# Graph convolution over 200,000 edges: feature parts stored once, a narrower spread of the source rows, and a zero fill moved from SP's queue to POOL's

## The chip, the cores and the metric

The kernel runs on one core of one Trainium2 chip. That core has five engines that run their own instruction streams: TensorE (PE, with its weight loads shown as PEld), VectorE (DVE), ScalarE (ACT), GpSimd (POOL) and SyncE (SP). SP computes nothing here; it issues most of the DMAs. POOL issues the DMAs that gather or scatter by index, and a few plain ones. The metric is the time of one execution in device microseconds (us), the median of several runs. Before the change it is 2110.86 us (three runs, 2110.19 to 2114.73).

## The reference: one message passing layer

There are 6250 nodes with 128 features each, and 200,000 edges. An edge has a source, a destination (the edges are sorted by it), 20 features and a weight. What is computed is, cut to its core:

```
h    = relu(layernorm(x))                      # 6250 x 128
xn   = h @ W_in                                # 6250 x 128
W_ij = (ssp(f_ij @ W_f1 + b_f1) @ W_f2 + b_f2) * cutoff     # one row of 128 per edge
m    = xn[dst] * W_ij                          # gather by idx_j = dst, 200,000 x 128
out  = segment_sum(m, idx_i = src, 6250)       # scatter-add by source
y    = x + ssp(out @ W_o1 + b_o1) @ W_o2 + b_o2
```

`ssp` is the shifted softplus, log(1+e^v) - log 2. The gather is by the sorted column, so it is local. The scatter-add is by the unsorted column, so it goes all over the 6250 rows.

## The kernel before, in words

**Quads.** The edges are cut in chunks of 128, and four chunks make a quad of 512 edges (391 quads). Two quads make a superchunk `s` of 1024 edges, the unit in which `load_sc(s)` (line 265) loads. The main loop (line 945) runs one iteration a quad, software pipelined by hand: iteration `i` does the first stage of quad `i`, the second of `i-1`, the scatter of `i-4`, and at even `i` issues `load_sc(i/2+2)`. Inside `manual_schedule` every engine executes its instructions in the order in which the Python code issues them. Work that happens only sometimes (preparing nodes, splitting features, zeroing, the permuted quads) hangs on hooks: `at(i, point, fn, ...)` puts it at a named point of iteration `i`.

**Edge filter.** For a quad, PE multiplies the split weights `ws` with the feature tile `ft` (`s1_pe`, L290). ACT and DVE make the softplus of it (L295 to L325), and PE multiplies by `W_f2` (L348). To keep float32 accuracy with bfloat16 products, every float32 feature is split into three bfloat16 parts (high, middle, low) and the weights likewise. `ft` has 6 groups of 20 rows: some parts of the features stand in it several times, beside different parts of the weights. Which weight part stands in which group is the table `part` (line 1267).

**The features' way.** Features are split in blocks of 4096 edges (49 of them; `fb_load`, `fb_1` to `fb_4`, L238 to L263). The result goes to the DRAM tensor `fsd` by three DMAs (L260 to L262), which store 6 copies: the high part three times, the middle part twice, the low part once. `load_sc` then reads `ft`, 120 rows of 1024 bfloat16, by one DMA (L271).

**Gather.** `wn` (L283) loads four windows of 21 rows, each with three bfloat16 parts, of the table of nodes `tab`, and a one-hot matrix made from `rb` (L276) picks rows out of them by a matmul (L340). ACT and DVE multiply with the filter to give the messages `m` (L353, L358).

**Scatter, two ways.** 60% of the quads, and all of the first eight, are *plain*: `sb` holds the row of source numbers spread over all 128 partitions (L273), DVE compares it with the sources as a column to get `eq` (L319), a matmul with `eq` (L370) adds up messages of the same source in a chunk, ACT copies the sum into one of five buffers `s` (L378), and POOL issues one scatter-add DMA a chunk, four a quad (L418). The other 40% (`mpi`: quads 8, 10, 13, 15, 18, 20 and so on) are *permuted*: they are sorted into bins by matmuls (L528) and added up in an on-chip accumulator `accT` by more matmuls (L621), with only one scatter-add for two quads. Permuted quads read no `sb`.

**Four accumulators.** Scatter-adds go to four DRAM accumulators in turn (`acc_of`, line 402): the first two scatters to accumulator 0, up to the eighth to 0 and 1, then to three and later to four. A scatter to an accumulator waits until the one before it to the same accumulator has landed. Before any of this an accumulator has to be zeroed, by ten DMAs of 320 KB (`zero_piece`, line 144). Accumulator 0 is zeroed by POOL (4 pieces at L674, 6 at L761). Accumulator 1 is zeroed by ten pieces that SP issues ahead of the main loop (L774). The pieces of accumulators 2 and 3 are spread over SP's first iterations.

**Queues.** SP executes its DMAs in order, and so does POOL. In the instruction listing a DMA of SP's gets one of eight semaphores in turn, so it also waits until the DMA eight places ahead of it has landed; the same holds for POOL's with eight semaphores of their own. One `load_sc` is 8 DMAs of SP's: `ft`, `sb`, two `rb`, four `wn`.

**The end.** After the loop a repair loop (L1008) runs zero times with these inputs. Then the three remaining accumulators are loaded (L1076), summed with `accT`, and go through the two output matmuls.

Of the kernel before, what the change touches and what calls it, by code (L numbers as in the profile page):

```python
# [8 lines left out]
BF16 = mybir.dt.bfloat16  # L9
# [11 lines left out]
P = 128  # L21
SC = 1024
SEG = 512
# [16 lines left out]
HB = 64  # L40
NR = 3 * WIN
NACC = 4
CQ = 16
EARLY_N = 256

# [2 lines left out]
def tile_gnn(ctx: ExitStack, tc: tile.TileContext, x, fB, cT, srcT, srcr, dstr, win_, wf1, wf2, bias, bo1c, wo1,  # L48
             wo2, consts, ident, out, n_edges):
    nc = tc.nc  # L50
    N = out.shape[0]
    NP = x.shape[0]
    NB, RB, BE = fB.shape
    EP = NB * BE
    KF = 6 * RB
    K1 = KF + 3
    FE = RB * BE // P
# [12 lines left out]
    ZR = 10 if ACC_R % 10 == 0 else 1  # L70
# [4 lines left out]
    mpi = {q: n for n, q in enumerate(mpq)}  # L75
# [12 lines left out]
    dp = ctx.enter_context(tc.tile_pool(name="dp", bufs=1, space=DRAM))  # L88
# [6 lines left out]
    accs = []  # L95
    for k in range(NACC):
        a_ = dp.tile([ACC_R, P], F32, name=f"acc{k}")
# [1 line left out]
    tab = dp.tile([NP * 3, P], BF16, name="tab")  # L99
    reld = dp.tile([NSC, SC], BF16, name="reld")  # L100
    src16 = dp.tile([NSC, SC], I16, name="src16")
    fsd = dp.tile([NB, 6, RB * BE], BF16, name="fsd")
    dropd = dp.tile([P, EP // P], BF16, name="dropd")

    con = cp.tile([P, 16], F32, name="con")
# [38 lines left out]
    def zero_piece(eng, k, j, parts=1):  # L144
        v = accs[k].rearrange("(p t) f -> p (t f)", p=P).rearrange("p (r e) -> r p e", r=ZR)
        w = ACC_R // ZR // parts
        for h in range(parts):
            eng.dma_start(v[j][:, h * w:(h + 1) * w], zero[:, :w])
# [107 lines left out]
    def fb_4(b):  # L256
        f3 = fst[b]["f3"]
        nc.vector.tensor_tensor(f3[:, 2], fst[b]["fr"], f3[:, 1], op=ALU.subtract)
        v = fsd[b].rearrange("g (p e) -> p g e", p=P)
        nc.sync.dma_start(v[:, 0:3], f3[:, 0:1].to_broadcast([P, 3, FE]))  # L260
        nc.sync.dma_start(v[:, 3:5], f3[:, 1:2].to_broadcast([P, 2, FE]))
        nc.sync.dma_start(v[:, 5:6], f3[:, 2:3])  # L262
        del fst[b]  # L263

    def load_sc(s):
        n = min(SC, NQ * SEG - s * SC)
        pp, hh, nh = s % HALF, s // HALF, n // SEG
        top = caps[s]
        ft = fts[s % len(fts)]
        b, o = s * SC // BE, s * SC % BE  # L270
        nc.sync.dma_start(ft[:KF, :n], fsd[b].rearrange("g (r e) -> (g r) e", r=RB)[:, o:o + n])  # L271
        sb = ld.tile([P, SC], I16, tag="sb", name="sb")
        nc.sync.dma_start(sb[:, :n], src16[s:s + 1, :n].to_broadcast([P, n]))  # L273
        rb = ld.tile([P, SEG], BF16, tag="rb", name="rb")
        for j in range(nh):
            nc.sync.dma_start(rb[j * HB:(j + 1) * HB], reld[s:s + 1, j * SEG:(j + 1) * SEG].to_broadcast([HB, SEG]))  # L276
        wn = ld.tile([P, 2, P], BF16, tag="wn", name="wn")
        _, regs = nc.values_load_multi_w_load_instructions(
            base_i[pp:pp + 1, hh, 0:2 * nh], engines=[SP], min_val=0, max_val=top,
            skip_runtime_bounds_check_because="clamped on the chip to [0, top]")  # L280
        for k in range(2 * nh):
            j, c = divmod(k, 2)
            nc.sync.dma_start(wn[j * HB:j * HB + NR, c, :], tab[bass.ds(regs[k] * 3, NR), :])  # L283
        loads[s] = (ft, sb, rb, wn)
# [367 lines left out]
    def c_load(b):  # L652
        n = min(4 * CQ, EP // P - 4 * CQ * b)
        t_ = ld.tile([P, 4 * CQ], F32, tag="cb", name="cb", bufs=2)
# [16 lines left out]
    with tc.manual_schedule():  # L671
# [88 lines left out]
        nc.gpsimd.tensor_copy(b2rep, b2p.unsqueeze(1).to_broadcast([P, 4, P]))  # L760
        for j in range(ZR * 4 // 10, ZR):  # L761
            zero_piece(nc.gpsimd, 0, j)
        ms = []
        for i in range(2):
            m_ = cp.tile([P, 4, 132], F32, name=f"m{i}")
# [5 lines left out]
            load_sc(1)  # L771
        if NB > 1:
            fb_load(1)
        for j in range(ZR):  # L774
            zero_piece(nc.sync, 1, j)

        hooks = {}

        def at(i, point, fn, *a):
# [228 lines left out]
    with tc.For_i(0, trips, 1) as ci:  # L1008
        dcol = wk.tile([P, 1], I32, bufs=1, tag="dcol", name="dcol")
        nc.sync.dma_start(dcol, dstr.rearrange("s (e o) -> (s e) o", o=1)[bass.ds(ci * P, P), :])  # L1010
        rcol = wk.tile([P, 1], BF16, bufs=1, tag="rcol", name="rcol")
        nc.sync.dma_start(rcol, reld.rearrange("s (e o) -> (s e) o", o=1)[bass.ds(ci * P, P), :])
        scol = wk.tile([P, 1], I32, bufs=1, tag="scol", name="scol")
        nc.sync.dma_start(scol, srcr.rearrange("s (e o) -> (s e) o", o=1)[bass.ds(ci * P, P), :])
        ccol = wk.tile([P, 1], F32, bufs=1, tag="ccol", name="ccol")
        nc.sync.dma_start(ccol, cT[:, bass.ds(ci, 1)])
        xcol = wk.tile([P, 1], BF16, bufs=1, tag="xcol", name="xcol")
        nc.sync.dma_start(xcol, dropd[:, bass.ds(ci, 1)])
        sb = wk.tile([P, P], I32, bufs=1, tag="oeq", name="fsb")
        nc.sync.dma_start(sb, srcr.rearrange("s e -> (s e)")[bass.ds(ci * P, P)].unsqueeze(0).to_broadcast([P, P]))  # L1020
        ft = wk.tile([P, P], BF16, tag="oh", name="fft")
        nc.vector.memset(ft[96:P, :], 1.0)
        fsel = fsd.rearrange("b g (r e) -> b (g r) e", r=RB)
        nc.sync.dma_start(ft[:KF, :], fsel[bass.ds(ci // (BE // P), 1), :, bass.ds((ci % (BE // P)) * P, P)]
                          .rearrange("o m e -> (o m) e"))
        x3 = wk.tile([P, 3, P], BF16, tag="pt", name="fx3")
        nc.gpsimd.indirect_dma_start(out=x3.rearrange("p k f -> p (k f)"), out_offset=None,
                                     in_=tab.rearrange("(n k) f -> n (k f)", k=3),
                                     in_offset=bass.IndirectOffsetOnAxis(ap=dcol[:, 0:1], axis=0))
        ok = wk.tile([P, 4], F32, bufs=1, tag="ok", name="ok")  # L1030
        nc.vector.tensor_scalar(ok[:, 0:1], rcol, float(WIN), None, op0=ALU.is_ge)
        nc.vector.tensor_scalar(ok[:, 1:2], rcol, 0.0, None, op0=ALU.is_lt)
        nc.vector.tensor_tensor(ok[:, 2:3], ok[:, 0:1], ok[:, 1:2], op=ALU.add)
        nc.vector.scalar_tensor_tensor(ok[:, 3:4], ok[:, 2:3], xcol, ccol, op0=ALU.max, op1=ALU.mult)
        xw = wk.tile([P, P], F32, bufs=1, tag="rm", name="fxw")
        nc.vector.tensor_tensor(xw, x3[:, 0], x3[:, 1], op=ALU.add)
        nc.vector.tensor_tensor(xw, xw, x3[:, 2], op=ALU.add)
        z = ps.tile([P, P], F32, tag="A", name="fz", bufs=4)
        nc.tensor.matmul(z, ws, ft[:K1, :], start=True, stop=True)
        e = wk.tile([P, P], F32, tag="e", name="fe")  # L1040
        nc.scalar.activation(e, z, AF.Abs)
        nc.scalar.activation(e, e, AF.Exp, scale=-1.0)
        nc.scalar.activation(e, e, AF.Ln, bias=half, scale=0.5)
        a = wk.tile([P, P], F32, tag="a", name="fa")
        nc.vector.scalar_tensor_tensor(a, z, 0.0, e, op0=ALU.max, op1=ALU.add)
        W = ps.tile([P, P], F32, tag="A", name="fW", bufs=4)
        nc.tensor.matmul(W, onesb[HB:], b2rep[HB:, 0, :], start=True, stop=False)
        nc.tensor.matmul(W, a, w2, start=False, stop=True)
        m = wk.tile([P, 132], F32, tag="xc", name="fm")
        nc.vector.tensor_copy(m[:, 128:129], wgt)  # L1050
        nc.vector.scalar_tensor_tensor(m[:, :P], W, ok[:, 3:4], xw, op0=ALU.mult, op1=ALU.mult)
        eq = wk.tile([P, P], F32, tag="eq", name="feq")
        nc.vector.tensor_tensor(eq, sb, scol.to_broadcast([P, P]), op=ALU.is_equal)
        pp = ps.tile([P, 132], F32, tag="B", name="fpp", bufs=4)
        nc.tensor.matmul(pp[:, :129], eq, m[:, :129], start=True, stop=True)
        s = wk.tile([P, P], F32, bufs=1, tag="dg", name="fs")
        nc.scalar.copy(s, pp[:, :P])
        dlt = wk.tile([P, 2], F32, bufs=1, tag="dlt", name="dlt")
        nc.vector.tensor_scalar(dlt[:, 0:1], scol, trash, None, op0=ALU.subtract)
        nc.vector.scalar_tensor_tensor(dlt[:, 1:2], pp[:, 128:129], wgt2, dlt[:, 0:1], op0=ALU.is_lt, op1=ALU.mult)  # L1060
        ji = wk.tile([P, 1], I32, bufs=1, tag="fji", name="fji")
        nc.vector.tensor_scalar(ji, dlt[:, 1:2], trash, None, op0=ALU.add)
        nc.gpsimd.indirect_dma_start(out=accs[1][:, :], out_offset=bass.IndirectOffsetOnAxis(ap=ji[:, 0:1], axis=0),
                                     in_=s, in_offset=None, compute_op=ALU.add)
# [172 lines left out]
def _layout(inputs):  # L1237
    import numpy as np

    p = "L0_gnn_"  # L1240
# [3 lines left out]
    n, e = x.shape[0], src.shape[0]  # L1244
# [19 lines left out]
    con[:, 14] = np_ // GRP // 2 - con[:, 3]  # L1264
    con[:n_sc // 2, 5] = caps[:n_sc // 2]
    con[:n_sc // 2, 6] = caps[n_sc // 2:]
    part = np.array([0, 1, 2, 0, 1, 0])
    for r in range(6 * rb + 3):
        con[r, 7 + (part[r // rb] if r < 6 * rb else r - 6 * rb)] = 1.0
    for r in range(3):  # L1270
# [39 lines left out]
```

## Time and profile before

| What | us |
|---|---|
| median of three runs | 2110.86 |
| the profiled execution | 2108.97 |
| its span, from the first instruction to the last | 2107.2 |
| PE busy in the span | 1926.4 (91%) |
| ACT busy | 1793.4 (85%) |
| DVE busy | 1774.3 (84%) |
| POOL busy | 1685.2 (80%) |
| share of the 16 DMA engines, SP's queue | 39.4% |
| share of the 16 DMA engines, POOL's queue | 34.8% |
| bytes moved | 314.79 MB |

The busy share of an engine is an average over the start (to about 110 us), the steady loop and the end (from about 2000 us), which have different limits. POOL's busy time leaves out the short stretch between two of its DMAs in which nothing is recorded as waited for; the idle column of its rows shows it. A row of a timeline gives start, duration, and in square brackets the idle time before it with what ended it. A wait for several things is put down to the one that came last.

### The profile page before, as it was taken

What the parts mean: (1) busy time and instruction counts of PE and PEld (TensorE: products, weight loads), DVE (VectorE), ACT (ScalarE), POOL (GpSimd) and SP (SyncE); (2) the same over time, 40 slices, a digit from 0 to 9 for tenths busy, and PEclk for the clock granted to TensorE, in tenths of its full rate; (3) what the DMA queues carried; (4) which work ended last, traced back from release to release, by engine and by line L of the source; (5) the groups of instructions that cost most, each with busy time, mean ns of one, the idle gap of its engine ahead of it and who ended that gap; (6) DMA issues with size and microseconds to landing.
All of it is one profiled execution on the core that took longest, in us unless ns stands there. A gap on an engine that the chain in (4) does not pass through costs nothing. (4 is left out here: it accounts for less than half of the span.)

```text
span 2107.2 us, 56868 instructions
## 1 busy us (share of the span) xinstructions
PE 1926.4 (91%) x19917; PEld 1402.2 (67%) x19917; DVE 1774.3 (84%) x4749; ACT 1793.4 (85%) x4789; POOL 1685.2 (80%) x1067
## 2 busy tenths in 40 slices
PE   3788999999999999999999999999999999999976
PEld 2566666676767666766666677777777766766644
DVE  4767888888889898888888989898988988888855
ACT  4687988898989898988889999989899889988824
POOL 2677878888888888888887888888888888888874
PEclk9888999999999999999999999999999999999997
DMA  7986767777777777777776777777777777777739
GB/s 266 237 179 126 153 133 144 135 155 137 152 136 154 141 140 147 152 141 141 152 142 140 144 140 135 152 140 150 137 152 149 142 138 143 138 132 161 138 39 240
DMA packets 394833, 314.79 MB, mean 149 GB/s; under 512 B 94863, under 2 KB 334266, under 8 KB 394546
## 3 DMA queue, kind: packets, MB, share of 16 engines
q1 hardware_dynamic: 245858, 240.57, 39.4%
q0 software_dynamic: 148400, 70.52, 34.8%
q8 instruction: 156, 2.56, 0.5%
q14 instruction: 131, 1.07, 0.2%
q10 hardware_dynamic: 288, 0.07, 0.0%
HBM read 173.32 MB, written 137.67 MB: 148 GB/s over the span
## 5 line engine op out<-in xcount | busy, mean ns | idle before, releaser
L418 POOL DMA_INDIRECT acc<-s,ji x948 | 1523.7, 1607 | 348.1 <-issue 225.6
L528 PE MATMUL pq<-pt,pm 128*128 128x387 bf16 x2464 | 487.0, 337 | 32.9 <-ACT s L378 18.7
L353 ACT ACTIVATE xc<-xg,cb 128x128 f32<-128x128 f32 x1564 | 446.5, 374 | 64.7 <-PE xg L340 50.1
L348 PE MATMUL W<-w,a 128*128 128x128 f32 x3128 | 462.5, 292 | 0.0
L348 PEld LDWEIGHTS W<-w,a 128*128 128x128 f32 x3128 | 386.9, 195 | 41.7 <-issue 2.0
L621 PE MATMUL un<-so,mst 32*128 32x392 bf16 x7392 | 359.4, 329 | 35.1 <-DVE pr L468 14.8
L528 PEld LDWEIGHTS <-pm 128*128 128x128 bf16 x2464 | 241.2, 98 | 195.3 <-issue 40.3
L621 PEld LDWEIGHTS <-mst 32*128 32x128 bf16 x7392 | 227.1, 94 | 162.3 <-issue 63.4
L325 DVE SCALAR_TENSOR_TENSOR a<-z,e 128x512 f32<-128x512 f32 x391 | 266.9, 683 | 64.9 <-ACT e L301 37.1
L301 ACT ACTIVATE e<-e,con 128x512 f32<-128x512 f32 x391 | 282.3, 722 | 12.7
L370 PEld LDWEIGHTS pp<-m,eq 128*128 128x128 f32 x1896 | 254.5, 196 | 32.6 <-DVE accT L632 13.7
L370 PE MATMUL pp<-m,eq 128*128 128x129 f32 x1896 | 260.8, 281 | 12.4 <-DVE accT L632 9.0
L534 ACT CAST mst<-pq 128x387 bf16<-128x387 f32 x616 | 264.2, 481 | 6.2 <-PE pq L528 4.7
L295 ACT ACTIVATE e<-z 128x512 f32<-128x512 f32 x391 | 241.7, 618 | 18.5 <-PE z L290 17.8
L296 ACT ACTIVATE e<-e 128x512 f32<-128x512 f32 x391 | 246.5, 630 | 12.4
L378 ACT COPY s<-pp 128x258 f32<-128x258 f32 x474 | 165.2, 391 | 91.2 <-DMA acc<-s,ji 34.4
L358 DVE TENSOR_TENSOR m<-W,xc 128x512 f32<-128x512 f32 x237 | 162.3, 685 | 69.7 <-ACT xc L353 49.6
L518 DVE TENSOR_TENSOR pt<-pt 128x512 f32<-128x512 f32 x308 | 212.5, 690 | 0.0
L504 DVE TENSOR_SCALAR pm<-iot,pos 128x576 bf16<-128x576 f16 x616 | 202.0, 389 | 0.0
L358 DVE TENSOR_TENSOR pt<-W,xc 128x512 f32<-128x512 f32 x154 | 105.9, 687 | 81.2 <-ACT xc L353 50.5
L632 DVE TENSOR_TENSOR accT<-un,accT 128x392 f32<-128x392 f32 x288 | 142.8, 557 | 36.9 <-PE un L621 26.2
L290 PE MATMUL z<-ft,ws 123*128 123x512 bf16 x391 | 152.2, 390 | 18.3 <-DMA ft<-fsd 18.3
(156 smaller groups left out, 2710.6 us busy)
## 6 DMA issues: line engine op xcount, KB each, us to landing
sb<-src SPq DMA_DIRECT2D x195, 256.0 KB
ft<-fsd SPq DMA_DIRECT2D x195, 240.0 KB
rb<-reld SPq DMA_DIRECT2D x391, 64.0 KB
fsd<-f SPq DMA_DIRECT2D x49, 480.0 KB
fb<-in_fB_dram SPq DMA_DIRECT2D x49, 320.0 KB
fsd<-f SPq DMA_DIRECT2D x49, 320.0 KB
acc<-s,ji POOLq DMA_INDIRECT x948
wn<-tab SPq DMA_DIRECT2D x782, 15.8 KB
```

Source lines behind the costliest of these rows:

```text
L295: nc.scalar.activation(e, st[q]["z"], AF.Abs)
L296: nc.scalar.activation(e, e, AF.Exp, scale=-1.0)
L301: nc.scalar.activation(e, e, AF.Ln, bias=half, scale=0.5)
L325: nc.vector.scalar_tensor_tensor(a, st[q]["z"], 0.0, st[q]["l"], op0=ALU.max, op1=ALU.add)
L348: nc.tensor.matmul(W[:, c, :], st[q]["a"][:, c * P:(c + 1) * P], w2, start=False, stop=(c == 3))
L353: nc.scalar.mul(xc[:, c, :], st[q]["xg"][:, c, :], late["c", q // CQ][:, 4 * (q % CQ) + c:4 * (q % CQ) + c + 1])
L358: nc.vector.tensor_tensor(m[:, :, :P], st[q]["W"], st[q]["xc"], op=ALU.mult)
L370: nc.tensor.matmul(pp[:, c, :129], st[q]["eq"][:, k, :], m[:, k, :129], start=True, stop=True)
L418: nc.gpsimd.indirect_dma_start(out=accs[k][:, :], out_offset=bass.IndirectOffsetOnAxis(ap=ji, axis=0), in_=s, in_offset=None, compute_op=A ...
L528: nc.tensor.matmul(t[:, :PW], mp[q]["pm"][:, c, s * P:(s + 1) * P], high(mp[q]["pt"][:, c:c + 1, :PW])[:, 0], start=(c == 0), stop=(c == 3))
L534: nc.scalar.copy(mp[q]["ms", s][:, :PW], mp[q].pop(("q", s))[:, :PW])
L621: nc.tensor.matmul(ts[g][:, :GN], mp[q]["ms", s][v, k * P:(k + 1) * P], mp[q]["oh"][v], start=(q == qs[0] and k == 0), stop=(q == qs[-1] a ...
```

## The change

Three edits are made together.

1. `fsd` holds each of the three feature parts once. `fb_4` writes them by one DMA of 480 KB instead of three of 480, 320 and 160 KB. `load_sc` reads `ft` by three DMAs of 60, 40 and 20 rows: parts 0 to 2, then 0 and 1, then 0. The groups of `ft` now stand in the order 0 1 2 0 1 0, so the weights' table is turned to `[0, 0, 0, 1, 1, 2]`. The repair loop's load is changed in the same way.
2. `sb` is loaded only over the columns of the plain quads of the superchunk: 512 columns where one of its two quads is permuted, 1024 where both are plain.
3. The ten zero pieces of accumulator 1 are issued by POOL, right behind its last pieces of accumulator 0, and no more by SP ahead of the loop.

```diff
+FPARTS = ((0, 3), (3, 2), (5, 1))
-    fsd = dp.tile([NB, 6, RB * BE], BF16, name="fsd")
+    fsd = dp.tile([NB, 3, RB * BE], BF16, name="fsd")
...
     def fb_4(b):
         f3 = fst[b]["f3"]
         nc.vector.tensor_tensor(f3[:, 2], fst[b]["fr"], f3[:, 1], op=ALU.subtract)
-        v = fsd[b].rearrange("g (p e) -> p g e", p=P)
-        nc.sync.dma_start(v[:, 0:3], f3[:, 0:1].to_broadcast([P, 3, FE]))
-        nc.sync.dma_start(v[:, 3:5], f3[:, 1:2].to_broadcast([P, 2, FE]))
-        nc.sync.dma_start(v[:, 5:6], f3[:, 2:3])
+        nc.sync.dma_start(fsd[b].rearrange("g (p e) -> p g e", p=P), f3)
         del fst[b]
...
-        nc.sync.dma_start(ft[:KF, :n], fsd[b].rearrange("g (r e) -> (g r) e", r=RB)[:, o:o + n])
+        for g, m in FPARTS:
+            nc.sync.dma_start(ft[g * RB:(g + m) * RB, :n],
+                              fsd[b, :m].rearrange("g (r e) -> (g r) e", r=RB)[:, o:o + n])
         sb = ld.tile([P, SC], I16, tag="sb", name="sb")
-        nc.sync.dma_start(sb[:, :n], src16[s:s + 1, :n].to_broadcast([P, n]))
+        own = [j for j in range(nh) if 2 * s + j not in mpi]
+        if own:
+            v = slice(own[0] * SEG, (own[-1] + 1) * SEG)
+            nc.sync.dma_start(sb[:, v], src16[s:s + 1, v].to_broadcast([P, len(own) * SEG]))
...
         for j in range(ZR * 4 // 10, ZR):
             zero_piece(nc.gpsimd, 0, j)
+        for j in range(ZR):
+            zero_piece(nc.gpsimd, 1, j)
...
         if NB > 1:
             fb_load(1)
-        for j in range(ZR):
-            zero_piece(nc.sync, 1, j)
...
-    part = np.array([0, 1, 2, 0, 1, 0])
+    part = np.array([0, 0, 0, 1, 1, 2])
```

More of the change, by code (lines that the diff above doesn't have):

```diff
@@ L1023, in tile_gnn @@
         fsel = fsd.rearrange("b g (r e) -> b (g r) e", r=RB)
-        nc.sync.dma_start(ft[:KF, :], fsel[bass.ds(ci // (BE // P), 1), :, bass.ds((ci % (BE // P)) * P, P)]
-                          .rearrange("o m e -> (o m) e"))
+        for g, m in FPARTS:
+            nc.sync.dma_start(ft[g * RB:(g + m) * RB, :], fsel[bass.ds(ci // (BE // P), 1), :m * RB,
+                                                               bass.ds((ci % (BE // P)) * P, P)]
+                              .rearrange("o m e -> (o m) e"))
         x3 = wk.tile([P, 3, P], BF16, tag="pt", name="fx3")
```

## Prediction, made before the changed kernel was run

> **What bounds the kernel now.** I first read POOL's row on the page, its waits, and its timeline in the middle of the loop.
>
> ```profile
> L418 POOL DMA_INDIRECT acc<-s,ji x948 | 1523.7, 1607 | 348.1 <-issue 225.6
> ```
> ```profile
> POOL acc L418 <- issue: 234.1, 756, 3.4
> POOL acc L418 <- DMA acc<-s,ji: 41.5, 76, 4.9
> POOL acc L418 <- ACT ji L399: 30.8, 16, 23.6
> ```
> ```profile
> 1232.29 1.56 POOL L418 DMA_INDIRECT acc<-s,ji  x1 [0.30 <-issue]
> 1234.16 1.54 POOL L418 DMA_INDIRECT acc<-s,ji  x1 [0.30 <-issue]
> 1236.00 1.67 POOL L418 DMA_INDIRECT acc<-s,ji  x1 [0.30 <-issue]
> ```
>
> POOL shows 80% busy, but between two scatters it always spends 0.30 us that belong to no wait. A scatter thus costs about 1.9 us, and they stand back to back. Then the stages:
>
> ```profile
> 200.00:2000.00 1800.00, 1717.42 (x18258) 1249.61 (x18257) 1586.84 (x4264) 1618.74 (x4354) 1502.55 (x934) 1.00 0.75 144
> ...
> 2050.00:2107.00 57.00, 35.27 (x201) 24.52 (x193) 29.74 (x49) 25.34 (x39) 24.13 (x20) 0.81 0.88 226
> ```
>
> From 200 to 2000 us POOL is busy 1502.55 us with 934 operations; with 0.30 us each (280) that is 1783 of 1800. PE is close behind with 1717. So POOL sets the pace: the time is the first scatter's start (48.82), 1025 scatters (948 and 77 of the permuted quads), their waits, and an end of about 58 us from POOL's last scatter (2048.7). The DMA engines stand at 0.75 and bound nothing in the steady loop. Last, the start, on POOL, SP and PE:
>
> ```profile
> 48.82 1.65 POOL L418 DMA_INDIRECT acc<-s,ji  x1 [23.59 <-ACT ji L399]
> 55.37 1.95 POOL L418 DMA_INDIRECT acc<-s,ji  x1 [4.90 <-DMA acc<-s,ji]
> 62.12 1.54 POOL L418 DMA_INDIRECT acc<-s,ji  x1 [4.79 <-DMA acc<-accT]
> ```
> ```profile
> 25.39 1.23 SPq L271 DMA_DIRECT2D ft<-fsd  x1
> ...
> 32.73 7.58 SPq L148 DMA_DIRECT2D acc<-accT  x10
> 40.35 0.90 SPq L271 DMA_DIRECT2D ft<-fsd  x1
> ```
> ```profile
> 32.02 0.59 PE L290 MATMUL z<-ft,ws 123*128 123x512 bf16 x1 [2.51 <-DMA ft<-fsd]
> ...
> 37.09 0.39 PE L337 MATMUL W<-b2rep,onesb 64*128 64x512 bf16 x1
> ...
> 45.15 0.61 PE L290 MATMUL z<-ft,ws 123*128 123x512 bf16 x1 [6.58 <-DMA ft<-fsd]
> ```
>
> The chain to the first scatter is visible: SP's ten zero pieces (7.58 us) hold back the third `ft`; PE waits for it until 45.15; ACT makes the index `ji` behind that; POOL starts 3.67 us after PE's z.
>
> **The zero pieces.** SP loses 7.58 us ahead of the third `ft`. Against that, two more `ft` issues of the second load stand ahead of it, at 0.37 us (a plain SP issue, as the `fb` load at 32.00) to 1.23 us each: 0.7 to 2.5. The first load's two more issues (0.8) are covered by the wait for `src16`: its `ft` was issued at 18.47 and `sb` only at 20.44. The third `ft` itself ends 0.8 us later, being three issues. Its last part is issued at 40.35 - 7.6 + 0.7 + 0.8 = 34.3, at the latest 36.1. From issue to PE's start it took 4.8 us (40.35 to 45.15, beside SP's zeros) and for the second `ft` 6.6 (25.39 to 32.02, beside POOL's six pieces). That gives 39.1 to 42.7.
>
> But the bytes are still to be written, now beside the loads. In the stretch of POOL's last pieces the engines are full:
>
> ```profile
> 24.00:28.00 4.00, 1.23 (x6) 0.97 (x7) 2.33 (x4) 3.13 (x7) 1.23 (x3) 1.00 1.00 371
> ...
> 40.00:48.00 8.00, 2.85 (x15) 2.34 (x15) 1.06 (x3) 3.07 (x9) 0.00 (x0) 0.52 0.73 252
> ```
>
> At 371 GB/s ten more pieces (3.28 MB) take 8.8 us. If the loads shared evenly they would lose half of that, 4.4 us; if they waited for all of it, 8.8. The upper end for z is then 39.1 + 8.8 = 47.9, a loss of 2.8 us; the lower end 39.1 is a gain of 6.1. I take z at 42, near the second `ft`'s 6.6 us, which is the nearest row (loads beside POOL's pieces): the first scatter 3 us earlier, bounds 6.1 earlier to 2.8 later. POOL's issue of ten pieces costs nothing at 0.54 us each (six took 3.23): it stands idle for 23.59 us ahead of the first scatter. If that cover went, it would be 5.4 us.
>
> The Trainium skill ("DMA: Bandwidth & Descriptors", Issuing engines are not separate DMA queues) says that DMAs of SP, ACT and POOL run on the same 16 engines, and that issuing from another engine saves only issue time. The row at 24 us, full at 371 GB/s, does not contradict it. By it alone the whole 3.28 MB still stand in the loads' way, the first scatter gains nothing, and the sum would be 3 us smaller: 2107. By the rows I keep the 3 us.
>
> **The feature parts.** 49 x 480 KB fewer written, 98 fewer SP issues there and 390 more for `ft`. **The row of sources.** By the list of issues 153 of 195 `sb` loads shrink from 256 to 128 KB. Together 24.1 + 20.0 = 44 of 314.8 MB, 14%. What that is worth is read from POOL's waits for landings. Between 48.8 and 200 us POOL's idle times beyond 0.30 add up to 25.8 us over its timeline's rows; DMA stands at 0.94 from 48 to 110 us, and about 3.4 of 29 MB go (four blocks of `fsd`, a dozen `sb`). In proportion 12%, 3 us; bounds 0 (a landing may be all latency) and 8 (a third, queueing near full use). After 200 us the same excess is 13 us: 14% is 2, bounds 0 and 6. The duration above 1.54 us (68 us in all) I leave: from 60 to 110 us, with the engines fullest, the mean scatter is 1.59 us, in the loop at 0.75 it is 1.61, so it does not follow DMA load. Bounds for it 5 either way.
>
> SP's net 282 more issues (390 - 98 - 10) at 0.38 are 107 us of SP over the loop, 0.55 us a load. They are covered:
>
> ```profile
> SPq L273 <- DVE eq L319: 466.9, 113, 9.7
> ```
>
> SP waits 467 us for a free `sb` alone, and a load is issued four iterations (20 us) ahead of its use. Behind the later `ft` parts stand `sb`, `rb`, `wn` on SP; for them PE waits nowhere in the loop (all PE waits on `ft` are three, 18.3 us, at the start). If that cover went, 0.55 us a load would reach PE. PE's weight load of `ws` now waits for three landings instead of one; the additional semaphore instructions run ahead on PE's sequencer, as those before `oh` (L340) do, and the landings are long past: nothing, bounded above by 195 x 0.05 us = 10 were they serial. The single `fsd` write waits for DVE's last part, as L262 did (62.7 us of SP); it replaces two earlier waits of the same queue (L261, 61.4 us) and blocks SP until the same moment. `wk` buffers, DVE, ACT and PE work are unchanged.
>
> Another rule speaks against the three `ft` parts: the Trainium skill ("DMA: Bandwidth & Descriptors", Why a DMA increments its semaphore by 16 and not by 1) has a DMA run on the largest number up to 16 that divides both outer sizes, so 120 rows use 15 engines, and 60, 40, 20 rows use 15, 10, 10. Ten engines would carry 10 rows instead of 8. No row of this profile parts the DMA engines; by the rule a quarter more `ft` time on these engines would take back part of the 14%, and the waits' gain would be about 3 instead of 5 us.
>
> **Sum.** First scatter -3, early waits -3, later waits -2, durations 0: -8 us. PE must follow, with some 4% idle in the loop (1800 - 1717 = 83 us, only part of it POOL's doing), and the last PE and POOL work of the loop end together near 2050, so I count 1.5 us as lost to PE: -6.5. The profiled execution took 2108.97 (span 2107.2, 1.8 around it), so 2102.5 on its own scale; it lies 1.9 below the median of 2110.86, on which scale I predict 2104.
>
> **Rivals.** *Hidden:* the third `ft` arrives no earlier, because POOL's pieces take what SP's gave up, and landings are latency. For: bytes ahead of the first scatter hardly change. Against: PE's 6.58 us stall has SP's 7.58 directly ahead. Gain 0 to 3, time 2110. *Slower:* POOL's pieces starve the second load (`ft`, `rb`, `wn`) until all sixteen pieces have gone, about 22 + 14 = 36 us plus the loads' own 0.68 MB. Then z of the second load starts near 40.5 instead of 32.0; PE's way to the end of the next `W` (32.02 to 38.6) follows, z of the third load starts at 47, and the first scatters also queue behind zeros in POOL's own queue; at the 4.9 us that one landing costs now, one more such landing makes it about +7: 2118. It decides from the point where z of the third load starts later than 49.4, 4.2 us later than now. *Larger:* early waits go by half (13) and steady ones too (6), with 6 at the start: -25, but PE, 83 us off, stops some: 2093. *The rows change nothing* (`sb` and `fsd` off the path): contained in the first.
>
> **How the numbers follow.** Three runs spread over 0.2%, so 0.2% (4.2 us) is what a measurement can tell from no change. Forecast 0.48 (2098 to 2106.5), hidden 0.28, slower 0.16, larger 0.08. Faster: 0.48 + 0.08 = 0.56; same 0.28; slower 0.16. The likeliest one's own range is 2098 to 2106.5. For 8 in 10 I go from 2097 (leaving out most of "larger") to 2116 (leaving out the far half of "slower").
>
> **What would show it.** Right: on SP no ten-piece row at 32 us and the third `ft` issued by 36; PE's z of it at 39 to 43; the first scatter at 43 to 47; POOL's wait for `acc` landings below 41.5 us; fewer than 280 MB moved; loop rows of 1.54 + 0.30 unchanged. Wrong: the second `ft` landing well after 34 (starved), the first scatter after 49, waits of PE or DVE on `ft`, `rb`, `wn` in the loop (SP late), or a mean scatter that moves from 1607 ns, which I held independent of DMA load and which is worth 1 us for every ns.

## The result, and the profile after

The changed kernel takes 2102.74 us (median of 14 runs, 2094.84 to 2109.84) against 2115.19 for the kernel before (14 runs beside them, 2109.29 to 2121.47). The ratio is 0.9948, with a 95% interval of 0.9934 to 0.9962: some 11 us faster, give or take 3. The prediction was 2104 of 2110.86, a ratio of 0.9967, or 7 us. The direction was right, and the predicted ratio lies just outside the interval. Below, the runs show that two of the steps behind that sum did not go as written: the start was not won, and the saved bytes were worth more.

The profiled execution after took 2098.49 us with a span of 2096.7, against 2108.97 and 2107.2. From the page of the changed kernel, the bytes and POOL's row of scatters:

```profile
DMA packets 377588, 270.57 MB, mean 129 GB/s; under 512 B 97199, under 2 KB 337242, under 8 KB 377298
...
L421 POOL DMA_INDIRECT acc<-s,ji x948 | 1523.7, 1607 | 327.6 <-issue 217.8
```

44.2 MB are gone, as worked out. The scatters' mean is the same in these two profiles (1607 ns; over the profiles of all kernels below it lies between 1599 and 1614, in no order of the bytes moved). POOL's idle time ahead of them fell from 348.1 to 327.6 us. Of these 20.5 us, 5.5 are the idle time ahead of the first scatter, which zero pieces now fill, and are no gain. The other 15 lie between scatters.

POOL's timeline of the changed kernel at the start (start, duration, and in brackets the idle time before with what ended it) shows where the first scatter went:

```profile
22.00 5.88 POOL L149 DMA_DIRECT2D acc<-accT  x11
...
50.86 1.81 POOL L421 DMA_INDIRECT acc<-s,ji  x1 [18.11 <-ACT ji L402]
```

It starts at 50.86 instead of 48.82: 2 us **later**. SP's timeline and PE's of the same kernel say why:

```profile
18.40 1.12 SPq L270 DMA_DIRECT2D ft<-fsd  x3
...
25.71 3.72 SPq L270 DMA_DIRECT2D ft<-fsd  x3
...
35.61 3.27 SPq L286 DMA_DIRECT2D wn<-tab  x4
38.93 0.40 SPq L241 DMA_DIRECT2D fb<-in_fB_dram  x1
39.38 1.17 SPq L270 DMA_DIRECT2D ft<-fsd  x3
```
```profile
35.15 0.58 PE L293 MATMUL z<-ft,ws 123*128 123x512 bf16 x1 [5.72 <-DMA ft<-fsd]
...
43.90 0.38 PE L343 MATMUL xg<-wn,oh 63*128 63x128 bf16 x4 [1.96 <-DMA sb<-src]
...
46.07 0.63 PE L293 MATMUL z<-ft,ws 123*128 123x512 bf16 x1
```

The three `ft` issues of the second load take 3.72 us of SP, those of the first load 1.12, and its `wn` are issued only at 35.61. PE gets the second `ft` at 35.15 (before 32.02). The row at 43.90 names a landing of `sb`, but `xg` reads no `sb`; what had just ended, at 43.84, is ACT's `xc`, which empties the tile that `xg` fills (in e1 below the same row of PE names it). ACT's timelines, after and before, show what held it up:

```profile
42.08 0.72 ACT L246 CAST f<-fb 128x640 bf16<-128x640 f32 x1 [4.30 <-DMA fb<-in_fB_dram]
42.71 1.13 ACT L356 ACTIVATE xc<-xg,cb 128x128 f32<-128x128 f32 x4
```
```profile
35.06 0.73 ACT L245 CAST f<-fb 128x640 bf16<-128x640 f32 x1 [0.40 <-DMA fb<-in_fB_dram]
```

In ACT's order the cast of the next block of features stands ahead of `xc`. Its load `fb` comes behind the whole second load on SP, and was issued at 38.93 instead of 32.00. So the late second load holds PE twice, by its `ft` and by the `fb` behind it. The third `ft` was meant to be freed from SP's ten pieces; it is issued at 39.38 where it was issued at 40.35, and its z starts at 46.07 without any wait for it, because PE is late by then. Of the 2.0 us, 0.9 are this z's; from z to the scatter it takes 4.79 us instead of 3.67, as ACT, late too, still has an `xc` to do in between.

So the gain was made after the first scatter. Matching the scatters of the two profiles by their number, and subtracting starts (negative: the changed kernel is ahead):

| scatter number | start before, us | after minus before, us |
|---|---|---|
| 0 | 48.8 | +2.0 |
| 8 | 75.9 | 0.0 |
| 24 | 115.1 | -4.8 |
| 60 | 190.3 | -6.8 |
| 140 | 351.6 | -10.0 |
| 190 | 448.5 | -9.7 |
| 490 | 1022.4 | -7.6 |
| 790 | 1600.1 | -11.5 |
| 1024, the last | 2047.0 | -13.3 |

Most of the lead, 9.7 of 13.3 us, is there at 450 us; after that it wavers between 6 and 14. These are single profiles: a mean scatter that is 1 ns longer is worth 1 us at the end, and the 1599 to 1614 ns above show how far that goes. The windows of the two profiles (stage; its length; busy time and instructions of PE, PEld, DVE, ACT, POOL; granted clock; DMA share; GB/s) show it as work done. Before:

```profile
45.00:450.00 405.00, 357.21 (x3304) 263.62 (x3305) 324.48 (x881) 339.13 (x917) 310.39 (x191) 0.93 0.77 161
450.00:2000.00 1550.00, 1480.34 (x15756) 1077.80 (x15754) 1368.70 (x3671) 1396.18 (x3751) 1297.75 (x809) 1.00 0.75 144
```

After:

```profile
45.00:450.00 405.00, 364.04 (x3450) 270.64 (x3448) 334.57 (x917) 350.56 (x950) 316.52 (x197) 0.94 0.73 140
450.00:2000.00 1550.00, 1482.79 (x15715) 1080.89 (x15711) 1367.46 (x3666) 1396.44 (x3757) 1302.29 (x810) 1.00 0.70 121
```

Up to 450 us, 197 scatters instead of 191 and 950 ACT instructions instead of 917. After that, 810 and 809, though the DMA engines are relieved there by more (0.75 to 0.70) than before it (0.77 to 0.73).

At the end some is given back: from the end of the last scatter to the end of the span 61.4 us, before 58.5. SP's loads of the accumulators start 6.9 us after the last scatter's end (2035.33), before 3.9 us; what is late now is DVE's last addition to `accT`, at 2043.55 (before 2053.88, 5.2 us behind the scatters; now 8.2). From the start of that addition to the end of the span it is the same in both, 53 us.

### The profile page after: what moved, and what is told of

Read it like the earlier page. It is cut to its first block, busy times and chain, and to the rows that moved or that the text cites. A ratio compares the mean times of both kernels' runs of the same rounds, so it can differ in the third digit from the quotient of the medians.

```text
span 2096.7 us, 57222 instructions
## 1 busy us (share of the span) xinstructions
PE 1925.7 (92%) x19917; PEld 1404.4 (67%) x19917; DVE 1770.8 (84%) x4749; ACT 1792.0 (85%) x4789; POOL 1690.0 (81%) x1077
## 2 busy tenths in 40 slices
DMA packets 377588, 270.57 MB, mean 129 GB/s; under 512 B 97199, under 2 KB 337242, under 8 KB 377298
## 5 line engine op out<-in xcount | busy, mean ns | idle before, releaser
L421 POOL DMA_INDIRECT acc<-s,ji x948 | 1523.7, 1607 | 327.6 <-issue 217.8
L624 PE MATMUL un<-so,mst 32*128 32x392 bf16 x7392 | 358.7, 331 | 38.2 <-DVE pr L471 14.9
L293 PE MATMUL z<-ft,ws 123*128 123x512 bf16 x391 | 152.1, 389 | 14.9 <-POOL b2rep L763 9.2
```

Of the source, the lines that this page charges most:

```text
L421: nc.gpsimd.indirect_dma_start(out=accs[k][:, :], out_offset=bass.IndirectOffsetOnAxis(ap=ji, axis=0), in_=s, in_offset=None, compute_op=A ...
L624: nc.tensor.matmul(ts[g][:, :GN], mp[q]["ms", s][v, k * P:(k + 1) * P], mp[q]["oh"][v], start=(q == qs[0] and k == 0), stop=(q == qs[-1] a ...
```

## Experiments

All are timed beside the kernel before on the same chip, with a 95% interval of the ratio. First scatter, lead and idle times are from one profile of each.

### One edit at a time

**e1_zero** is the kernel before with edit 3 alone:

```diff
             zero_piece(nc.gpsimd, 0, j)
+        for j in range(ZR):
+            zero_piece(nc.gpsimd, 1, j)
...
-        for j in range(ZR):
-            zero_piece(nc.sync, 1, j)
```

> The kernel before with the third edit alone: POOL issues the ten zero pieces of accumulator 1, nothing else is changed. Theory 'early bytes' (the gain is made between about 90 and 350 us, where fewer bytes let the scatters land sooner): no gain here, ratio to before 0.999 to 1.002, the first scatter 2 to 4 us later than the 48.8 us of before, because the second load stands beside POOL's pieces. Rival 'zero move' (SP, rid of ten pieces, is ahead from then on, and that makes the gain): ratio near 0.995. Rival 'all over' (every byte less helps in the whole loop): 1.000, as no byte goes.

Measured: 2106.43 against 2108.85, ratio 0.9989 [0.9975, 1.0002]; the first scatter at 51.74, 2.9 us late. PE's timeline of this kernel, z of the second and the third load:

```profile
33.87 0.59 PE L290 MATMUL z<-ft,ws 123*128 123x512 bf16 x1 [4.28 <-DMA ft<-fsd]
...
47.14 0.63 PE L290 MATMUL z<-ft,ws 123*128 123x512 bf16 x1
```

As in the changed kernel, the second `ft` is late and the third z waits for no `ft` of its own, so the zero move alone makes this delay. By scatter 24 it is gone (0.1 us ahead). In time, moving the zeros is worth 2.3 us, give or take 2.8: these runs can tell it neither from no change nor from the 3 us that were predicted.

**e2_sb** is the kernel before with edit 2 alone:

```diff
-        nc.sync.dma_start(sb[:, :n], src16[s:s + 1, :n].to_broadcast([P, n]))
+        own = [j for j in range(nh) if 2 * s + j not in mpi]
+        if own:
+            v = slice(own[0] * SEG, (own[-1] + 1) * SEG)
+            nc.sync.dma_start(sb[:, v], src16[s:s + 1, v].to_broadcast([P, len(own) * SEG]))
```

> The kernel before with the second edit alone: sb is loaded only over plain quads; 20 MB less, none of it before superchunk 4. 'Early bytes': about 1.5 of the 3.4 MB that go before 200 us, so some 45% of the gain: ratio 0.997 to 0.998. 'Zero move': 1.000. 'All over': 20 of 44 MB, 0.9975, with the lead of the scatters growing evenly over the loop instead of before 350 us.

Measured: 2101.57, ratio 0.9967 [0.9951, 0.9982]; 294.61 MB. SP issues as many DMAs as before in this kernel (save one), so the gain is one of bytes and not of issues.

**e4_fsd** is the kernel before with edit 1 alone (cut to its core; the repair loop and `part` go with it):

```diff
-    fsd = dp.tile([NB, 6, RB * BE], BF16, name="fsd")
+    fsd = dp.tile([NB, 3, RB * BE], BF16, name="fsd")
...
-        v = fsd[b].rearrange("g (p e) -> p g e", p=P)
-        nc.sync.dma_start(v[:, 0:3], f3[:, 0:1].to_broadcast([P, 3, FE]))
-        nc.sync.dma_start(v[:, 3:5], f3[:, 1:2].to_broadcast([P, 2, FE]))
-        nc.sync.dma_start(v[:, 5:6], f3[:, 2:3])
+        nc.sync.dma_start(fsd[b].rearrange("g (p e) -> p g e", p=P), f3)
...
-        nc.sync.dma_start(ft[:KF, :n], fsd[b].rearrange("g (r e) -> (g r) e", r=RB)[:, o:o + n])
+        for g, m in FPARTS:
+            nc.sync.dma_start(ft[g * RB:(g + m) * RB, :n],
+                              fsd[b, :m].rearrange("g (r e) -> (g r) e", r=RB)[:, o:o + n])
```

> The kernel before with the first edit alone: feature parts written once, ft read by three DMAs; 24 MB less. 'Early bytes': 1.9 of the 3.4 MB before 200 us and a shorter burst of SP's writes, ratio 0.996 to 0.998; the first scatter as before or up to 2 us later (more ft issues). 'Zero move': 1.000 to 1.001. 'All over': 0.997, with an even growth of the lead.

Measured: 2101.0, ratio 0.9974 [0.996, 0.9988]; 290.75 MB. The first scatter starts at 50.63, 1.8 us late, by another way than in e1: the second z is in time (31.94), but the third `ft`, now three issues behind SP's zeros, is waited for. From PE's timeline:

```profile
46.98 0.59 PE L290 MATMUL z<-ft,ws 123*128 123x512 bf16 x1 [6.32 <-DMA ft<-fsd]
```

**e3_fsd_sb** has edits 1 and 2, which is the changed kernel with the zeros left on SP:

```diff
+        for j in range(ZR):
+            zero_piece(nc.sync, 1, j)
...
-        for j in range(ZR):
-            zero_piece(nc.gpsimd, 1, j)
```

> The first and second edit without the third: 44 MB less, and SP issues the zero pieces of accumulator 1 as before. 'Early bytes': the whole gain or more, ratio 0.993 to 0.995, the first scatter at 48 to 50 us. 'Zero move': 0.999 to 1.000. 'All over': 0.995, lead growing evenly.

Measured: 2099.35, ratio 0.9957 [0.9941, 0.9973], or 9 us give or take 3.4; 270.57 MB. The first scatter starts at 51.05, later than the 48 to 50 that were expected. With the zeros on POOL as well, in the changed kernel, it starts at 50.86: beside the other two edits the zero move shifts it by 0.2 us. The product of e3 and e1 is 0.9946, that of e1, e2 and e4 0.9930, and all three edits together gave 0.9948: within the intervals the edits add up, and the two that remove bytes carry most of the gain.

### Bytes put back, early or late

The bytes are removed over the whole loop. These kernels are the changed one with the bytes put back in a part of it: `sb` whole again, and the feature parts written a second time to a scratch tensor `bk` (480 KB a block, what edit 1 saved). 9.2 MB go back in **e5_back_early** (up to about 430 us by its timeline), 35 MB in **e6_back_late** (all after that).

```diff
         nc.sync.dma_start(fsd[b].rearrange("g (p e) -> p g e", p=P), f3)
+        if b <= 10:
+            nc.sync.dma_start(bk[b].rearrange("g (p e) -> p g e", p=P), f3)
...
-        own = [j for j in range(nh) if 2 * s + j not in mpi]
+        own = [j for j in range(nh) if 2 * s + j not in mpi or s < 40]
```

> The changed kernel with the bytes put back in the early part alone: for superchunks below 40 sb is loaded whole again, and for feature blocks up to 10 one more DMA writes 480 KB to a scratch tensor that nobody reads. About 9 of the 44 MB, all before some 410 us. 'Early bytes' (the gain is made between 90 and 450 us): most of the gain is gone, ratio to before 0.997 to 1.000. Rival 'all over' (bytes help in the whole loop): a fifth of it is gone, ratio 0.995 to 0.996.

Measured: 2106.08 against 2110.61, ratio 0.999 [0.9977, 1.0003]. A fifth of the bytes takes most of the gain away: 0.0042 of 0.0052.

e6 has `b > 10` and `s >= 40` instead:

```diff
+        if b > 10:
+            nc.sync.dma_start(bk[b].rearrange("g (p e) -> p g e", p=P), f3)
...
+        own = [j for j in range(nh) if 2 * s + j not in mpi or s >= 40]
```

> The changed kernel with the bytes put back in the late part alone: whole sb loads from superchunk 40 on, and one more write of 480 KB for every feature block above 10. About 35 of the 44 MB, all after some 410 us. 'Early bytes': the gain stays, ratio 0.994 to 0.996, the lead of the scatters at number 190 (about 440 us) as in the changed kernel and level after it. 'All over': four fifths of the gain are gone, ratio 0.998 to 1.000.

Measured: 2098.03, ratio 0.9948 [0.9932, 0.9964], the same as the changed kernel. 35 MB more, and nothing lost, give or take 4.5 us. The windows show the pair as mirror images (the same columns as above). e5:

```profile
45.00:450.00 405.00, 351.92 (x3314) 260.82 (x3313) 327.26 (x888) 341.45 (x926) 310.38 (x192) 0.94 0.77 160
450.00:2000.00 1550.00, 1482.85 (x15805) 1079.52 (x15804) 1369.98 (x3681) 1403.51 (x3765) 1302.09 (x811) 1.00 0.69 121
```

e6:

```profile
45.00:450.00 405.00, 360.39 (x3447) 266.71 (x3450) 336.39 (x914) 350.03 (x951) 314.65 (x197) 0.95 0.73 141
450.00:2000.00 1550.00, 1480.09 (x15723) 1079.30 (x15716) 1367.60 (x3669) 1397.92 (x3757) 1300.16 (x809) 1.00 0.75 144
```

With the DMA share at 0.77 in the first stretch there are 192 scatters, with 0.73 there are 197. In the second stretch 0.69 and 0.75 give 811 and 809. Leads at scatter 190: e5 1.8 us, e6 10.8, the changed kernel 9.7. The granted clock does not set this order: between 110 and 200 us it was 0.85 before and 0.89 in the changed kernel, but also 0.89 in e5, and 0.92 in e1, which gained next to nothing.

One row names who waits: ACT, for one of the five buffers `s` that a scatter still reads. From the groups of waits between 45 and 350 us (total us, times, longest), in the kernel before, after, e5 and e6 in this order:

```profile
ACT s L378 <- DMA acc<-s,ji: 23.3, 8, 5.5
```
```profile
ACT s L381 <- DMA acc<-s,ji: 11.0, 5, 5.6
```
```profile
ACT s L384 <- DMA acc<-s,ji: 20.4, 8, 7.2
```
```profile
ACT s L384 <- DMA acc<-s,ji: 11.7, 4, 7.0
```

### Which part of the early stretch

Two more kernels split e5. **e11_back_first** puts back 4.0 MB (`b <= 4`, `s < 18`, to about 200 us), **e12_back_mid** 5.2 MB (from there to about 425 us):

```diff
+        if b <= 4:
+            nc.sync.dma_start(bk[b].rearrange("g (p e) -> p g e", p=P), f3)
...
+        own = [j for j in range(nh) if 2 * s + j not in mpi or s < 18]
```

> The changed kernel with bytes put back up to about 200 us alone: whole sb loads below superchunk 18, and one more 480 KB write for feature blocks 0 to 4. About 4.0 MB. Narrow form: nearly all that the put-back below superchunk 40 took (ratio 0.999 there), 0.997 to 0.999. If any byte before 450 us counts alike: 4 of 9 MB, 0.9965 to 0.9975.

Measured: 2101.95 against 2107.55, ratio 0.997 [0.9957, 0.9984].

```diff
+        if 4 < b <= 10:
+            nc.sync.dma_start(bk[b].rearrange("g (p e) -> p g e", p=P), f3)
...
+        own = [j for j in range(nh) if 2 * s + j not in mpi or 18 <= s < 40]
```

> The changed kernel with bytes put back from about 190 to 410 us alone: whole sb loads from superchunk 18 to 39, one more 480 KB write for feature blocks 5 to 10. About 5.2 MB. Narrow form: the gain stays, 0.9945 to 0.996. If any byte before 450 us counts alike: 5 of 9 MB, 0.997.

Measured: 2102.58, ratio 0.9969 [0.9952, 0.9986]. Against 0.9948, e11 takes back 0.0022 and e12 0.0021; e5 took back 0.0042. The three point estimates add up, at about 1 us for a megabyte (8.9 us for 9.2 MB), and so does ACT's wait for a free `s` in the rows above: 15.7 us in e11, 14.9 in e12, between 11.0 and 20.4. That speaks for both halves counting. But the intervals do not exclude the narrow form, in which only the first 200 us count, and POOL's own rows lean to it: its idle time beyond 0.305 us, up to 400 us, is 29.6 us in e11 and 23.7 in e12, against 22.8 in the changed kernel.

### Does the first scatter's time matter?

**e7_zero_later** gives the second load its way back: the zeros of accumulator 1 stand on SP in the loop's second iteration, behind the third load.

```diff
-        for j in range(ZR):
-            zero_piece(nc.gpsimd, 1, j)
...
         for j in range(ZR):
+            at(1 if spread else 0, "L", zero_piece, nc.sync, 1, j)
+        for j in range(ZR):
             at(Z2[j] if spread else 0, "L", zero_piece, nc.sync, 2, j)
```

> The changed kernel with the zero pieces of accumulator 1 taken from POOL and issued by SP behind the loads of the half pieces (in iteration 1), so neither SP nor POOL's queue is in the way of the second and third load. If the starved second load costs what the first scatter lost: z of the third load near 39 to 41 us instead of 46.07, the first scatter at 43 to 46 instead of 50.86, ratio to before 0.991 to 0.994. If the first scatter's start does not matter because the next scatters wait for landings anyway: 0.994 to 0.996. The fourth superchunk's ft comes behind the ten pieces; if that holds PE, 0.997.

Measured: 2100.72 against 2110.61, ratio 0.9956 [0.994, 0.9972]. POOL's timeline of this kernel:

```profile
45.31 2.10 POOL L421 DMA_INDIRECT acc<-s,ji  x1 [20.06 <-ACT ji L402]
...
79.09 1.83 POOL L421 DMA_INDIRECT acc<-s,ji  x1 [7.25 <-ACT e L299]
```

The first scatter starts at 45.31, 3.5 us earlier than before, in the middle of what had been predicted for the change. But scatter 8, the first to accumulator 2, follows an idle time of 7.25 us and is 3.2 us late: SP's zeros stand ahead of the next loads and the pieces of accumulator 2. PE is idle for 7.43 us ahead of it, up to 72.88, until an `ft` lands. The start that was won is lost eight scatters later, to the zeros in their new place. Of the two ratios that were expected, the one without a gain from the start (0.994 to 0.996) came.

**e8_zero_sooner** does the opposite: POOL issues its sixteen pieces some 9 us earlier, ahead of the first load.

```diff
         src_cast(0, 0, SC, nc.gpsimd, "pt")
+        for j in range(ZR * 4 // 10, ZR):
+            zero_piece(nc.gpsimd, 0, j)
+        for j in range(ZR):
+            zero_piece(nc.gpsimd, 1, j)
...
-        nc.gpsimd.tensor_copy(b2rep, b2p.unsqueeze(1).to_broadcast([P, 4, P]))
+        nc.scalar.copy(b2rep, b2p.unsqueeze(1).to_broadcast([P, 4, P]))
```

> The changed kernel with POOL's six last pieces of accumulator 0 and its ten of accumulator 1 issued at about 14.4 us, right behind its cast of the sources, instead of 22 us; the copy that makes b2rep goes to ACT. DMA stands at 0.55 to 0.65 from 12 to 24 us, so the pieces fill idle time and are through by about 30 us. If bytes ahead of the second and third load set the first scatter: it comes at 45 to 48 us, ratio 0.992 to 0.994. If the first load is starved instead: z of quad 0 from 22.2 to 24 to 27 us, the first scatter at 50 to 53, ratio 0.995 to 0.997.

Measured: 2099.01, ratio 0.9957 [0.9942, 0.9972]. PE's timeline, the first z of the kernel (before: at 22.24), and POOL's, the first scatter:

```profile
32.66 1.01 PE L293 MATMUL z<-ft,ws 123*128 123x512 bf16 x2 [19.62 <-DMA ft<-fsd]
```
```profile
53.11 2.14 POOL L421 DMA_INDIRECT acc<-s,ji  x1 [27.15 <-ACT ji L402]
```

PE starts 10 us late and POOL 4.3 us late, yet the lead at scatter 190 is 11.5 us and the time is that of the changed kernel. The first load was starved more than feared (z at 24 to 27 us had been named for that case). First scatters at 45.3, 50.9 and 53.1 give 0.9956, 0.9948 and 0.9957. The 5.5 us that e7's scatter starts ahead of the changed kernel's do not carry to the end. The 2.3 us of e8 lie within the intervals; there the profile alone, with its lead back by scatter 140 (9.6 us), speaks for a loop that recovers. Neither run moves the start without also moving zeros into another stretch.

### A version that relieves the early stretch further

If early bytes cost, the ten pieces of accumulator 3 should be spread later. **e9_third_later** is the changed kernel with this, **e10_before_third_later** the kernel before with it:

```diff
-    Z2, Z3 = [0,0,1,1,2,2,3,3,4,4], [5+2*j for j in range(10)]
+    Z2, Z3 = [0,0,1,1,2,2,3,3,4,4], [20+3*j for j in range(10)]
```

In both, the pieces that come late fill accumulator 3 with other data than zeros, because they are copied from a part of `accT` that holds sums by then; their number, size and places are as stated, but the result is not the layer's.

> The changed kernel with the ten zero pieces of the last accumulator (number 3, first used by scatter 143 near 345 us) put on iterations 20 to 47 (about 140 to 280 us) instead of 5 to 23 (60 to 157 us). No byte less, only 3.3 MB later. 'Early bytes' in its narrow form (what counts is the stretch to about 200 us, DMA at 0.9): another 1 to 4 us, ratio to before 0.993 to 0.9945. If any byte before 450 us counts alike: as the changed kernel, 0.9948.

Measured: 2094.93 against 2107.55, ratio 0.9937 [0.9914, 0.996].

> The kernel before with that shift alone: no byte less, none of the three edits. Narrow form: ratio 0.997 to 0.999. If any byte before 450 us counts alike: 1.000. If the time depended on the number of bytes alone and not on when: 1.000.

Measured: 2105.39, ratio 0.9989 [0.9971, 1.0006].

Both point to some 2 us against the kernel without the shift; neither interval excludes none. These runs do not show that the shift beats the changed kernel.

## Why the prediction was right or wrong, step by step

**What bounds the kernel: right up to the last scatter.** The scatters sum to 1648.5 us (before 1648.9), and the lead at the last scatter is what POOL's stretches add up to: 2.0 us lost at the start, 15.0 won between scatters, 13.0 in sum and 13.3 in the profile. The end hangs on PE's and DVE's last work: DVE's last addition comes 10.3 us sooner, and the span is 10.5 us shorter.

**"The zero pieces": wrong in the mechanism.** This is the step that failed. It took z of the third load at 42, by the 4.8 to 6.6 us that an `ft` took from issue to PE; it started at 46.07, and the first scatter came 2.0 us late instead of 3 us early. The stated far end (47.9, 2.8 us late) was nearly reached. What the sum left out is that PE does not come to the third load while the second is late, and that the `fb` behind the second load is late with it, for which ACT waits 4.30 us. Its term for SP was mis-sized too. The second load's three `ft` issues took 3.72 us, at the end of what it had allowed for them, but `sb`, `rb` and `wn` behind them were left as before and took 9.4 us instead of 5.3; so the third `ft` was not issued at 34.3, at the latest 36.1, but from 39.38 to 40.55. The rival "slower" had this mechanism: z of the second load starved (35.15, where it feared 40.5), PE's way behind it following, z of the third load at 47. Its fear was overdone, as it put the second load behind all sixteen pieces, and its price of 7 us did not come.

What became of the 3 us is less clear than the mechanism. e1 measures the move at 2.3 us, give or take 2.8, and the changed kernel lies 1.9 us below e3, give or take 4.5, so a gain of up to 3 is not excluded; but it is not made where it was credited. In e1 a first scatter 2.9 us late is made up for by scatter 24, and in e7 one that is 3.5 us early has lost its lead at scatter 8. The start is not a term that can simply be added to the rest.

The Trainium skill ("DMA: Bandwidth & Descriptors", Issuing engines are not separate DMA queues) was weighed in the prediction: read by it alone, the first scatter gains nothing from pieces that are issued elsewhere. The runs agree as to the first scatter: 2.9 us late in e1, and 0.2 us ahead of e3 in the changed kernel.

**"Early waits" and "later waits": the right mechanism, mis-sized.** They were set at 3 and 2 us, in proportion to the bytes, 5 in all; edits 1 and 2 alone measured 9, give or take 3.4 (e3), and putting the early bytes back cost 8.9, give or take some 4 (e5). Over POOL's rows the idle time beyond 0.305 us fell from 38.9 us to 23.8; up to 400 us from 32.9 to 22.8, with the bytes alone (e3) to 25.0, and with the early bytes put back (e5) it is 30.5. Between 110 and 400 us it fell from 15.5 to 10.7 (e3 8.6, e5 16.5), about a third, where the bytes in a microsecond fell by 12 to 14% (154 to 135 and 141 to 121 GB/s). One profile each is a rough measure: e10, with no byte less, has 10.6 there. Up to 110 us it fell from 17.4 to 12.1, but neither bytes alone (16.4 in e3) nor the zero move alone (15.6 in e1) do that; why the three together do is open. Proportion was the error. The bound of 8 up to 200 us held (25.8 to 18.1), that of 6 after it did not in this pair of profiles (13.1 to 5.7). The place was off as well: "after 200 us" was credited to the whole loop, and by e5 and e6 nearly all of it belongs ahead of some 430 us.

**"POOL's wait for `acc` landings below 41.5 us": wrong as a sign.** The whole group stands at 42.7 us after. Between 100 and 400 us the part beyond 0.305 us of the rows that name a landing of `s` fell from 7.4 to 4.2, but it is 6.3 in e6, which has the same early bytes and the same time, and 8.9 in e5. The better sign is ACT's wait for a free `s`, which halved and came back in e5.

**SP, the three `ft` parts, PE's wait for three landings: costed at nothing, right.** From the waits of SP in the changed kernel:

```profile
SPq L276 <- DVE eq L322: 323.2, 86, 8.8
SPq L260 <- DVE f L259: 187.3, 40, 9.9
```

The cover of 466.9 us is now 323.2 ahead of `sb`, and 187.3 ahead of the single `fsd` write, which took over the waits of two. In the loop PE waits for no `ft`. As for the skill's rule, by which the three parts use 15, 10 and 10 engines (same page, Why a DMA increments its semaphore by 16 and not by 1), no run here parts the DMA engines; e4 alone, at 0.9974, shows only that its cost does not eat up the gain. Only at the start did the three parts cost something: e4's first scatter is 1.8 us late.

**Scatter durations independent of DMA load: right**, 1607 ns at 314.79 and at 270.57 MB. That the two are equal to the nanosecond is luck: e1 has 1604 at 314.79 MB, e2 1599 at 294.61, e3 1612 at 270.57, and e11 1614 at 274.60.

**1.5 us taken back by PE: not measured.** In this pair of profiles 2.9 us went at the end, behind DVE's last `accT`, which is fed by PE. But from the last scatter to the end the kernels take between 58.4 and 63.2 us in no order of their times, and e6, as fast as the changed kernel, takes 58.4.

**The sum** of 6.5 us thus came near 11 partly by luck: the 3 us for an earlier start, which did not come, stood beside a gain from bytes that was priced at about half.

**What stays open** is why a byte costs only in the first 400 us or so. POOL's rows narrow it down: up to scatter 140, at 351.6 us, only two or three accumulators rotate, and POOL's idle time beyond 0.305 us ends there. In the kernel before it is 5.3 us from 250 us to scatter 142, and 0.0 from scatter 143, the first to the fourth accumulator, to 450 us; in e5 6.0 and 0.2, although its extra bytes go on to 430 us. From 450 to 800 us it is 0.1 in both, and over the whole rest some 6 us before, 1 in the changed kernel and 4 in e6: little is left that fewer bytes could shorten, and what there is lies within the intervals. The likeliest reason is argued and was not tried: with a scatter each 1.85 us a landing has an estimated 5.5 us before its accumulator is wanted again with three in rotation, and 7.4 with four, so a landing that traffic delays reaches POOL's path in the first case only. No run changes the scatter at which the fourth comes in. Nor do the runs part the extra bytes of e5 from its eleven extra issues on SP (about 0.6 us each); e6 has 38 such issues, all late, and e2 gains without a change in issues.

## What to carry to other kernels

Price saved bytes by stage: put them back in one stretch at a time, for here 9 MB in the first 430 us were worth 9 us and 35 MB later nothing that could be measured, at nearly the same DMA share. Look first for waits that the bytes can shorten: where POOL had next to none left, fewer bytes won nothing measurable. Do not scale waits in proportion to traffic; between 110 and 400 us, at shares of 0.73 to 0.75, 12 to 14% fewer bytes took off about a third of them. And before a start that comes earlier is credited, ask what stands behind it: with the first scatter between 45 and 53 us the kernels took the same time within 2 us.

## What was not expected of the hardware

POOL's stream of 320 KB pieces crowds out SP's smaller loads, down to their issue. In the windows of the changed kernel (columns as above) the engines are full through both rows, at 368 and 369 GB/s, where the second row before had 0.87 and 237 GB/s:

```profile
24.00:28.00 4.00, 1.31 (x7) 1.05 (x8) 2.33 (x4) 3.16 (x8) 3.88 (x8) 1.00 0.99 368
28.00:32.00 4.00, 1.43 (x7) 1.13 (x6) 2.46 (x3) 0.60 (x3) 2.16 (x4) 1.00 1.03 369
```

In that stretch three `ft` issues took 3.72 us of SP; with six pieces instead of sixteen (e4) they took 2.71, and ahead of the pieces 1.12. The load arrived 3 us later than before. In e8, with all sixteen pieces ahead of the first load, PE's first z came 10 us later.

The other is how little of a DMA share decides: 0.77 against 0.73 between 45 and 450 us was worth 2 to 3% more scatters (195 in e3 and 197, against 191 to 193), and 0.75 against 0.70 after it none.
